# State-layer keys rotated by a permutation product, with new planner settings, in a three-layer decoder kernel

## The chip, the cores and the metric

The kernel runs on one NeuronCore of a Trainium2 chip. The metric is the device time of one execution in microseconds (us). The core has four compute engines that run their own instruction streams in order and wait for each other through semaphores: PE (TensorE, matrix products into PSUM), DVE (VectorE), ACT (ScalarE) and POOL (GpSimd). SP issues the transfers. PEld is the loading of PE's stationary operand.

## What is computed

Two batches of 512 tokens with 1024 features go through three layers, each added to its input after a layer norm:

```python
x = x + _L0_attn_ref(_layernorm(x), ...)               # 32 heads, binarised weights
x = x + _L0_xattn_ref(_layernorm(x), pos, ..., ctx)    # the state layer
x = x + _L0_ffn_ref(_layernorm(x), ...)                # dense with low-rank terms
```

The change lies in the state layer's attention. It reads three vectors of 256 features per token, projects them to queries, keys and values of 16 heads by 16 features, and rotates queries and keys by the token's position:

```python
def rope(x, pos):
    half = HD // 2
    ...
    x1, x2 = (x[..., :half], x[..., half:])
    return concatenate([x1 * cos - x2 * sin, x2 * cos + x1 * sin], axis=-1)
q, k = rope(q, pos), rope(k, pos)
scores = where(causal, einsum(q, k) / 4, -1e30); o = softmax(scores) @ v
```

After it, `rat_write` mixes the result into the token's 1024 features by a recurrence of exponentials and softplus, a second read feeds a gated product with `ctx`, and a second `rat_write` follows. The numbers are float32.

## The kernel before

**The planner.** The kernel is written as jobs (Python generators). A job yields an engine, an estimated duration and a ready time before it emits the instructions of a step. `run` (L453) picks, over and over, the job whose step could start first, where a job's lag (us) is added to that start: a low lag lets a job go first. The order in which steps are picked is the program order on every engine, which the hardware then keeps. The estimated durations and lags are no waits: they only set the order. The list in `build` (L1688) gives each job its lag and its needs, the marks in `self.when` that must have been planned before it may begin. `spawn` (L508) starts a sub-job with the parent's lag plus an entry of `LAGS` (L432), looked up as job.function, then function, then -0.3. `take` and `give` (L524) hand out rooms of buffers that all jobs share: 2 PSUM banks ("bank"), 3 PSUM pairs of banks ("pair"), 12 slabs, 4 probs, 8 pages, 11 rows.

**The stages.** In the order of the profile: the first layer's weights and projections; for batch A (0) and B (1) the score maxima (maxA, maxB) and the attention (attA, attB); the output product (outA, outB), which stores the residual in DRAM (`kept`). Then the state layer: state_inputs (stateA, stateB), the maxima of its causal scores (maxC, maxD), attention (attC, attD), and tails (tailA, tailB: both `rat_write`s and what is between them). Last, denseA and denseB. Jobs of both batches overlap.

**state_inputs** (L1109). For each of four tiles of 128 tokens it loads `kept`, measures mean and variance (`measured`, L982), normalises on DVE, keeps the mean and factor in `norm` for the tails (two more DVE instructions of 128x1), and calls `read` (L999), which transposes, multiplies by the read weights, normalises the three outputs of 256 (one DVE instruction each), transposes back and applies gain and bias (`gained`, L1078). Batch A reads "wide" through pairs and probs, batch B through banks. When all four tiles are read, twelve products follow, each into a bank: four groups of 128 slots for queries (kind 0), keys (kind 1) and keys of a third, slot-permuted weight (kind 2). A group has four heads of 32 slots; each head stands in four runs of 8. `rotated` (L1147) multiplies a bank by one of three tables (`rotation_table`, L954) on DVE; for kind 2 it then adds the result to the keys of kind 1. So a rotated key is (weight 1 product) x cos + (weight 2 product) x signed sin. Four value products end the stage.

**Maxima and attention.** `peaks` (L554) multiplies queries by keys and reduces maxima on DVE. `turned` (L592) splits each negative maximum into three bf16 parts by four small DVE instructions, transposes them on PE and copies them to a `shift` row on ACT. `attend` (L618) multiplies again, adds the shift by a product with `ones16`, and takes exponentials on ACT. In the first layer the probabilities are added up on DVE, except in a group's last step when `direct` (L734) is true, which `SPARE` governs.

**The end.** tail_weights (L1355) loads the tails' weights and `ctx`, tail (L1376) handles 128 tokens (at most three at once, the "lanes"), dense_weights (L1536) adds a low-rank product to the dense weights on PE and DVE, dense (L1583) handles 128 tokens of the last layer.

Of the kernel before, what the change touches and what calls it, by code (L numbers as in the profile page):

```python
# [18 lines left out]
P = 128  # L19
# [50 lines left out]
class Kernel:  # L70
# [79 lines left out]
    def constants(self):  # L150
        nc = self.nc
        self.ident = self.const([P, P], "ident")
        make_identity(nc, self.ident)
        self.ident16 = self.const([P, P], "ident16", BF16)
        nc.vector.tensor_copy(self.ident16, self.ident)
        self.ones = self.const([P, P], "ones")
        nc.gpsimd.memset(self.ones, 1.0)
        self.ones16 = self.const([P, P], "ones16", BF16)
        nc.gpsimd.memset(self.ones16, 1.0)

        self.late = []
# [12 lines left out]

        self.spread = self.const([P, P], "spread")
        nc.vector.tensor_copy(
            self.spread.rearrange("p (j i) -> p j i", j=4),
            self.ident.rearrange("p (j i) -> p j i", j=4)[:, :, 16:17].to_broadcast([P, 4, 32]),
        )
        self.eps = self.const([P, 1], "eps")  # L180
        nc.gpsimd.memset(self.eps, EPS)

        self.eye = self.const([P, 32], "eye")
        nc.vector.tensor_reduce(
            self.eye, self.ident.rearrange("p (j r) -> p r j", j=4), AX.X, ALU.add
        )
# [238 lines left out]
    def output_weights(self):  # L425
# [8 lines left out]
        "attB.added": 0.0, "attB.ahead": -0.3, "co.emptied": -0.1, "cv.emptied": -0.1, "denseA.emptied": -1.0,  # L434
        "denseA.stored": 1.0, "denseA.summed": -0.6, "denseB.emptied": 0.3, "denseB.stored": -2.0,
        "denseB.summed": -0.1, "emptied": -0.6, "exponentials": 0.3, "factor.put": -1.0, "finished": 0.0,
        "gained": -1.0, "gated": -1.0, "joined": -0.6, "k.scale_of": 0.0, "maxA.reduced": 0.0,
        "maxA.turned": -0.1, "maxB.reduced": 0.3, "maxB.turned": -0.3, "maxD.turned": -0.3, "outA.clean": 1.0,
        "outA.stored": 2.0, "outB.stored": -1.0, "proj0.featured": -1.0, "proj0.valued": -0.6,
        "proj1.featured": -1.0, "proj1.valued": -0.6, "q.scale_of": 0.0, "residual": 1.0, "rotated": 0.0,  # L440
        "stateA.emptied": -0.3, "stateA.rotated": -0.1, "stateB.gained": 0.0, "stateB.rotated": 0.0,
        "stored": 0.6, "summed": -0.6, "tableB.emptied": -2.0, "tailA.gained": -1.0, "tailA.residual": -2.0,
        "tailB.emptied": -0.6, "tailB.gained": -2.0, "tailB.gated": 0.0, "tailB.residual": 0.3,
        "v.scale_of": 0.0, "weights.joined": -0.1, "wo.scale_of": 0.0,
    }
    SPARE = 1
# [145 lines left out]
    def turned(self, name, b, g, mx, reduced, earlier):  # L592
        nc = self.io
        yield from self.join(*earlier)
        t = yield from self.join(*reduced)
        t = yield "DVE", 1.2, t
        parts = self.parts[self.flip]
# [4 lines left out]
        nc.vector.tensor_copy(parts[:, :, :, 1], rest)  # L602
        nc.vector.tensor_tensor(parts[:, :, :, 2], rest, parts[:, :, :, 1], ALU.subtract)
# [14 lines left out]
    def attend(self, groups, operands, scale, causal):  # L618
# [24 lines left out]
        def probabilities(g, kt):  # L643
# [10 lines left out]
            for j in range(4):  # L654
                r = slice(32 * j, 32 * j + 3)
                self.mm(
                    s[j // 2][:, j % 2, q0:], lhsT=self.ones16[r, :], rhs=shift[r, q0:], start=False, stop=True
# [340 lines left out]

    def read(self, x, t, w, gb, nout, dst, wide):  # L999
# [59 lines left out]
        t = yield "DVE", 0.42 * nout, t  # L1059
        for o in range(nout):  # L1060
            nc.vector.tensor_scalar(
                rows[o], rows[o], mv[:, o, 0:1], rstd[:, o : o + 1], ALU.subtract, ALU.mult
            )
# [30 lines left out]
    def state_weights(self):  # L1094
# [7 lines left out]
        self.proj = [w[0][:, 0], w[0][:, 1], w[1][:, 0]]  # L1102
# [6 lines left out]
    def state_inputs(self, b, wide):  # L1109
# [10 lines left out]
        def tile_of(q):  # L1120
# [24 lines left out]
        firsts = {}  # L1145

        def rotated(bank, kind, g, dst, t):  # L1147
            if dst is None:
                yield from self.join(firsts[g])
                t = max(t, (yield from self.take("row")))  # L1150
            t = yield "DVE", 0.69, t
            to = self.row([P, S]) if dst is None else dst[:, g, :]
            nc.vector.tensor_tensor(to, bank, table[:, kind, :], ALU.mult)
            self.give("bank", t)
            if dst is None:
                t = yield "DVE", 0.69, t
                nc.vector.tensor_tensor(kk[:, g, :], kk[:, g, :], to, ALU.add)
                self.give("row", t)
# [3 lines left out]
        for kind, (y, dst) in enumerate(((ys[0], qq), (ys[1], kk), (ys[1], None))):  # L1162
            w = self.proj[kind]
            for g in range(4):
                room = yield from self.take("bank")
                done = yield "PE", 1.9, max(t, room)
                bank = self.bank([P, S])
                self.accumulate(bank, [(w[:, i, g * P : (g + 1) * P], y[:, i, :]) for i in range(2)])
                job = self.spawn(rotated(bank, kind, g, dst, done))
                ends.append(job)  # L1170
                if kind == 1:
                    firsts[g] = job
# [515 lines left out]
    def build(self):  # L1688
# [39 lines left out]
                ("stateA", self.state_inputs(0, True), 0.2, "attB.scores"),  # L1728
# [62 lines left out]
def _layout(inputs):  # L1791
# [16 lines left out]
                _slots(qkv[1], (1, 0, 1, 0)),  # L1808
# [39 lines left out]
```

## Time and profile before

| | |
|---|---|
| median of 3 runs | 1129.61 us (1126.38 to 1132.65) |
| profiled execution | 1127.92 us |
| its span, first to last instruction | 1126.2 us |
| mean granted PE clock | 0.96 |

Times in the profile count from the first instruction. Where the stages lie (first to last instruction on PE, us):

| stage | PE | stage | PE |
|---|---|---|---|
| attB | 431 to 533 | maxD | 721 to 776 |
| outB | 533 to 592 | attD | 769 to 841 |
| stateA | 541 to 622 | tailA | 722 to 981 |
| stateB | 611 to 721 | weights | 842 to 859 |
| maxC | 622 to 668 | tailB | 877 to 1081 |
| attC | 661 to 709 | denseA, denseB | 868 to 1103, 982 to 1122 |

How to read the rows: a group row has the line of the code, engine, operation, what it writes and reads with shapes, the count, the busy time and the mean of one in ns, then the idle time of the engine before it with what ended it. A row of a timeline or of the chain begins with start and duration in us. A float32 product appears as two MATMUL records. Almost every instruction carries the line of a helper (L51, L130, L133, L142), so rows are told apart by tile names: `stateA_bank` is a PSUM bank of job stateA. A PE that is called busy is not at its peak, since the ends of products are modelled; the granted clock (1.00 is full) stands beside it.

### The profile page before, as it was taken

The page shows a single profiled execution, that of the slowest core. Times are in us where ns is not written, and L with a number is a line of the kernel's source. Part 1 is how long each engine was busy: PE and PEld are TensorE (multiplying, and loading weights), DVE is VectorE, ACT ScalarE, POOL GpSimd, SP SyncE. Part 2 cuts the span into 40 slices and gives each one's busy share as a digit, 9 for nine tenths or more (in the row PEclk, how much of TensorE's full clock was granted, in tenths as well). Part 3 has the DMA queues.
Part 4 walks back from the last instruction along what each step waited for, and adds up shares of the span by engine and source line. Part 5 has one row for each costly group of instructions (what it writes and reads, how often), then busy time and mean ns, then how long its engine had stood idle before and what let it go on. Part 6 is the DMA issues. An engine that isn't in the chain of part 4 may idle for free.

```text
span 1126.2 us, 16121 instructions
## 1 busy us (share of the span) xinstructions
PE 1056.2 (94%) x6364; PEld 520.5 (46%) x6364; DVE 840.2 (75%) x1391; ACT 443.9 (39%) x714; POOL 238.2 (21%) x249
## 2 busy tenths in 40 slices
PE   4889999999999998999999899989988999998998
PEld 3554353333233632332554553546455466664643
DVE  8978888578888856787877972499758778687751
ACT  6762101388600214787121256225753233432210
POOL 3542333411321403364452012001210000000000
PEclk8999999999998998999999899969999999987999
DMA  6621000100214221150012200510131101111100
GB/s 255 211 78 29 20 10 20 29 20 23 63 38 145 118 75 38 31 199 1 28 68 74 94 1 1 228 38 1 51 144 50 50 7 57 38 38 38 38 19 38
DMA packets 25520, 70.51 MB, mean 63 GB/s; under 512 B 5330, under 2 KB 5348, under 8 KB 24548
## 3 DMA queue, kind: packets, MB, share of 16 engines
q1 hardware_dynamic: 25444, 69.48, 18.0%
q8 instruction: 50, 0.82, 0.3%
q14 instruction: 26, 0.21, 0.1%
HBM read 50.59 MB, written 10.49 MB: 54 GB/s over the span
## 4 chain that ended last, share of the span: by engine, by line
PE 78%; DVE 13%; ACT 5%; issue 2%; DMA 1%; POOL 1%; SPq 0%; DVEq 0%; ACTq 0%; POOLq 0%
PE proj_bank L130 8%; PE denseA_pair L130 6%; PE denseB_pair L130 5%; PE outA_bank L130 4%; PE attA_pair L130 4%; PE attB_pair L130 4%; PE tailA_bank L130 4%; PE attA_bank L130 3%; PE attB_bank L130 3%; PE maxB_pair L130 3%; PE maxA_pair L130 3%; PE outB_bank L130 3%; PE stateB_bank L130 3%; PE tailB_bank L130 3%; PE factor_bank L130 3%; PE tailA_pair L130 2%
## 5 line engine op out<-in xcount | busy, mean ns | idle before, releaser
L51 DVE TENSOR_REDUCE maxB_mx<-maxB_pair 128x2 f32<-128x1024 f32 x64 | 75.4, 1219 | 21.2 <-PE maxB_pair L130 21.0
L51 DVE TENSOR_REDUCE maxA_mx<-maxA_pair 128x2 f32<-128x1024 f32 x64 | 75.6, 1216 | 14.1 <-PE maxA_pair L130 14.1
L130 PEld LDWEIGHTS <-start_slab 128*128 128x128 bf16 x480 | 45.0, 99 | 69.8 <-issue 22.9
L51 DVE TENSOR_TENSOR attB_probs<-attB_probs,attB_probs 128x1024 f32<-128x1024 f32 x46 | 62.7, 1401 | 12.8 <-PE attB_bank L130 7.1
L51 ACT ACTIVATE attB_probs<-attB_pair 128x1024 f32<-128x1024 f32 x64 | 62.6, 1023 | 20.2 <-PE attB_pair L130 10.1
L51 DVE TENSOR_TENSOR attA_probs<-attA_probs,attA_probs 128x1024 f32<-128x1024 f32 x46 | 56.8, 1283 | 16.8 <-ACT attA_probs L51 9.8
L51 ACT ACTIVATE attA_probs<-attA_pair 128x1024 f32<-128x1024 f32 x64 | 62.0, 1021 | 9.8 <-PE attA_pair L130 9.4
L130 PE MATMUL proj_bank<-in_slab,start_slab 128*128 128x512 bf16 x240 | 57.0, 388 | 1.6 <-ACT in_slab L51 1.6
L130 PE MATMUL proj_bank<-in_probs,start_slab 128*128 128x512 bf16 x240 | 54.7, 380 | 0.0
L130 PE MATMUL maxB_pair<-maxB_row,proj_slab 32*128 32x512 f32 x256 | 47.9, 691 | 3.1 <-DVE maxB_mx L51 3.1
L51 POOL TENSOR_SCALAR proj_row<-proj_row 128x512 f32<-128x512 f32 x24 | 48.1, 2006 | 1.9
L130 PE MATMUL outA_bank<-wo_slab,attA_slab 128*128 128x512 bf16 x192 | 47.6, 398 | 0.7 <-ACT maxB_shift L51 0.7
L130 PE MATMUL attB_pair<-proj_slab,attB_row 32*128 32x512 f32 x256 | 46.9, 686 | 0.0
L51 ACT ACTIVATE proj_row<-proj_bank,cs 128x512 f32<-128x512 f32 x20 | 13.7, 686 | 81.8 <-PE proj_bank L130 61.2
L130 PE MATMUL outB_bank<-wo_slab,attB_slab 128*128 128x512 bf16 x192 | 43.3, 380 | 0.3 <-POOL attB_slab L51 0.3
L130 PE MATMUL attA_pair<-proj_slab,attA_row 32*128 32x512 f32 x256 | 41.6, 639 | 0.3 <-ACT attA_probs L51 0.3
L130 PE MATMUL attB_bank<-attB_probs,proj_slab 128*32 128x512 f32 x256 | 37.6, 619 | 1.1 <-DVE tableA_slab L51 0.7
L51 ACT COPY maxB_shift<-maxB_bank 128x512 bf16<-128x512 bf16 x8 | 4.7, 585 | 85.9 <-PE maxB_bank L133 85.9
L51 POOL TENSOR_SCALAR proj_slab<-proj_row 128x512 f32<-128x512 f32 x24 | 14.8, 616 | 107.7 <-ACT proj_row L51 89.1
L130 PE MATMUL maxA_pair<-maxA_row,proj_slab 32*128 32x512 f32 x256 | 36.8, 640 | 0.0
L51 POOL TENSOR_SCALAR_AFFINE_SELECT attD_probs<-attD_probs 128x512 f32<-128x512 f32 x16 | 12.0, 750 | 114.7 <-ACT attD_probs L51 105.2
L51 POOL TENSOR_SCALAR outA_row<-outA_row 128x512 f32<-128x512 f32 x16 | 21.4, 1340 | 65.0 <-DVE outA_row L51 60.8
(411 smaller groups left out, 2297.3 us busy)
## 6 DMA issues: line engine op xcount, KB each, us to landing
in_page<-in_x_dram SPq DMA_DIRECT2D x8, 512.0 KB, 3.9
q_page<-in_q_weight_dram SPq DMA_DIRECT2D x8, 512.0 KB, 5.4
wo_page<-in_o_weight_dram SPq DMA_DIRECT2D x8, 512.0 KB, 3.6
tailW_slab<-in_write_dram SPq DMA_DIRECT2D x3, 752.0 KB, 10.9
maxA_row<-proj_slab SPq DMA_DIRECT2D x32, 64.0 KB, 2.0
attA_row<-proj_slab SPq DMA_DIRECT2D x32, 64.0 KB, 2.0
maxB_row<-proj_slab SPq DMA_DIRECT2D x32, 64.0 KB, 2.0
outA_page<-in_x_dram SPq DMA_DIRECT2D x4, 512.0 KB, 3.8
```

The source lines that it names most:

```text
L51: return self.kernel.pin(getattr(self.engine, name)(*args, **kw))
L130: self.pin(self.nc.tensor.matmul(*args, **kw))
```

## The change

- The third key weight, its load and its four products per batch go. `keyed` takes its place: ACT copies the raw keys from the bank to a row, DVE multiplies the same bank by the cos table, PE multiplies the row by a 128x128 permutation `swap` (halves of each 16 slots exchanged) into another bank, DVE multiplies this by the sin table and adds it. Keys are computed first, queries after.
- `keep` (the `norm` pair) moves from DVE, after the normalisation, to POOL, before it. The normalisations go through `standard` with other estimated durations.
- `turned` splits the positive maximum; the sign moves to the constant: `minus16` for `ones16`.
- `LAGS`, `SPARE`, and lags and needs of jobs change.

```diff
@@ constants
-        self.ones16 = self.const([P, P], "ones16", BF16)
-        nc.gpsimd.memset(self.ones16, 1.0)
+        self.minus16 = self.const([P, P], "minus16", BF16)
+        nc.gpsimd.memset(self.minus16, -1.0)
...
+        self.swap = self.const([P, P], "swap")
+        halves = [t.rearrange("p (e h i) -> p e h i", h=2, i=8) for t in (self.swap, self.ident)]
+        for h in range(2):
+            nc.vector.tensor_copy(halves[0][:, :, h, :], halves[1][:, :, 1 - h, :])
@@ LAGS, only entries that differ
-        "denseA.emptied": -1.0, "denseA.stored": 1.0, "denseB.stored": -2.0, "denseB.summed": -0.1,
-        "rotated": 0.0, "stateA.rotated": -0.1, "stateB.rotated": 0.0,
-        "tailA.residual": -2.0, "tailB.gained": -2.0, "tailB.gated": 0.0,
+        "denseA.emptied": -2.0, "denseA.stored": -2.0, "denseB.stored": -0.1, "denseB.summed": -2.0,
+        "maxD.reduced": -0.3, "stateA.gained": -0.3,
+        "tailA.residual": 0.6, "tailB.gained": -0.1, "tailB.gated": -0.3,
-    SPARE = 1
+    SPARE = 100
@@ turned
-        nc.vector.tensor_scalar(parts[:, :, :, 0], mx, -1.0, None, ALU.mult)
-        nc.vector.scalar_tensor_tensor(rest, mx, -1.0, parts[:, :, :, 0], ALU.mult, ALU.subtract)
+        e.tensor_copy(parts[:, :, :, 0], mx)
+        e.tensor_tensor(rest, mx, parts[:, :, :, 0], ALU.subtract)
...
@@ new
+    def standard(self, parts, n, t):
+        t = yield "DVE", (0.15 + n / 1500) * len(parts), t
+        for x, mean, r in parts:
+            self.io.vector.tensor_scalar(x, x, mean, r, ALU.subtract, ALU.mult)
+        return t
@@ state_weights
-        for kind in range(3):
+        for kind in range(2):
             t = yield from self.fetch(self.proj[kind], a["proj"][:, kind], 512)
@@ state_inputs, tile_of
-            t = yield "DVE", 1.3, t
-            nc.vector.tensor_scalar(x, x, mv[:, 0, 0:1], r, ALU.subtract, ALU.mult)
             keep = self.small([P, 2], "norm", bufs=8)
-            nc.vector.tensor_copy(keep[:, 1:2], r)
-            nc.vector.tensor_scalar(keep[:, 0:1], mv[:, 0, 0:1], r, -1.0, ALU.mult, ALU.mult)
+            yield "POOL", 0.4, t
+            nc.gpsimd.tensor_copy(keep[:, 1:2], r)
+            nc.gpsimd.tensor_scalar(keep[:, 0:1], mv[:, 0, 0:1], r, -1.0, ALU.mult, ALU.mult)
+            t = yield from self.standard([(x, mv[:, 0, 0:1], r)], D, t)
@@ state_inputs, rotation
+        def keyed(bank, g, t):
+            tr = max(t, (yield from self.take("row")))
+            tr = yield "ACT", 0.59, tr
+            raw = self.row([P, S])
+            nc.scalar.copy(raw, bank)
+            t = yield "DVE", 0.69, t
+            nc.vector.tensor_tensor(kk[:, g, :], bank, table[:, 1, :], ALU.mult)
+            self.give("bank", max(t, tr))
+            room = yield from self.take("bank")
+            tr = yield "PE", 0.97, max(tr, room)
+            other = self.bank([P, S])
+            self.mm(other, lhsT=self.swap, rhs=raw, start=True, stop=True)
+            t = yield "DVE", 1.38, max(t, tr)
+            nc.vector.tensor_tensor(raw, other, table[:, 2, :], ALU.mult)
+            self.give("bank", t)
+            nc.vector.tensor_tensor(kk[:, g, :], kk[:, g, :], raw, ALU.add)
+            self.give("row", t)
+            return t
...
-        for kind, (y, dst) in enumerate(((ys[0], qq), (ys[1], kk), (ys[1], None))):
+        for kind, y in ((1, ys[1]), (0, ys[0])):
@@ build, lags and needs
-                ("stateA", self.state_inputs(0, True), 0.2, "attB.scores"),
+                ("stateA", self.state_inputs(0, True), 0.2, "attB.7"),
...
-                ("maxD", self.peaks_2(1, "stateB"), 0.5, "stateB", "attC.scores"),
-                ("tailW", self.tail_weights(), -0.5, "attC", "stateB"),
+                ("maxD", self.peaks_2(1, "stateB"), 0.5, "stateB"),
+                ("tailW", self.tail_weights(), -1.0, "attC"),
                 ("tailA", self.tails(0), 0.5, "attC", "tailW"),
-                ("attD", self.attend_2(1, "maxD"), 0.2, "maxD.1"),
-                ("weights", self.dense_weights(), -1.0, "attD"),
-                ("tailB", self.tails(1), 0.2, "attD", "tailW", "tailA.1"),
-                ("denseA", self.dense_all(0, "tailA"), 0.5, "tailA.0"),
-                ("denseB", self.dense_all(1, "tailB"), 0.5, "tailB.0"),
+                ("attD", self.attend_2(1, "maxD"), 0.2, "maxD", "attC"),
+                ("weights", self.dense_weights(), 0.5, "attD"),
+                ("tailB", self.tails(1), 0.0, "attD", "tailW", "tailA.1"),
+                ("denseA", self.dense_all(0, "tailA"), 0.2, "tailA.0"),
+                ("denseB", self.dense_all(1, "tailB"), 0.2, "tailB.0"),
```

More of the change, by code (lines that the diff above doesn't have):

```diff
@@ L433 @@
         "added": 0.0, "ahead": 0.0, "attA.ahead": -0.1, "attA.exponentials": -0.1, "attA.finished": 0.3,
-        "attB.added": 0.0, "attB.ahead": -0.3, "co.emptied": -0.1, "cv.emptied": -0.1, "denseA.emptied": -1.0,
-        "denseA.stored": 1.0, "denseA.summed": -0.6, "denseB.emptied": 0.3, "denseB.stored": -2.0,
-        "denseB.summed": -0.1, "emptied": -0.6, "exponentials": 0.3, "factor.put": -1.0, "finished": 0.0,
+        "attB.added": 0.0, "attB.ahead": -0.3, "co.emptied": -0.1, "cv.emptied": -0.1, "denseA.emptied": -2.0,
+        "denseA.stored": -2.0, "denseA.summed": -0.6, "denseB.emptied": 0.3, "denseB.stored": -0.1,
+        "denseB.summed": -2.0, "emptied": -0.6, "exponentials": 0.3, "factor.put": -1.0, "finished": 0.0,
         "gained": -1.0, "gated": -1.0, "joined": -0.6, "k.scale_of": 0.0, "maxA.reduced": 0.0,
[L438 to L444, printed above, removed]
+        "maxA.turned": -0.1, "maxB.reduced": 0.3, "maxB.turned": -0.3, "maxD.reduced": -0.3,
+        "maxD.turned": -0.3, "outA.clean": 1.0, "outA.stored": 2.0, "outB.stored": -1.0,
+        "proj0.featured": -1.0, "proj0.valued": -0.6, "proj1.featured": -1.0, "proj1.valued": -0.6,
+        "q.scale_of": 0.0, "residual": 1.0, "stateA.emptied": -0.3, "stateA.gained": -0.3,
+        "stateB.gained": 0.0, "stored": 0.6, "summed": -0.6, "tableB.emptied": -2.0, "tailA.gained": -1.0,
+        "tailA.residual": 0.6, "tailB.emptied": -0.6, "tailB.gained": -0.1, "tailB.gated": -0.3,
+        "tailB.residual": 0.3, "v.scale_of": 0.0, "weights.joined": -0.1, "wo.scale_of": 0.0,
     }
-    SPARE = 1
+    SPARE = 100
     def run(self, jobs):
@@ L596, in turned @@
         t = yield "DVE", 1.2, t
+        e = nc.vector
         parts = self.parts[self.flip]
@@ L599, in turned @@
         rest = self.small([P, NT, 4], "rest")
-        nc.vector.tensor_scalar(parts[:, :, :, 0], mx, -1.0, None, ALU.mult)
-        nc.vector.scalar_tensor_tensor(rest, mx, -1.0, parts[:, :, :, 0], ALU.mult, ALU.subtract)
-        nc.vector.tensor_copy(parts[:, :, :, 1], rest)
-        nc.vector.tensor_tensor(parts[:, :, :, 2], rest, parts[:, :, :, 1], ALU.subtract)
+        e.tensor_copy(parts[:, :, :, 0], mx)
+        e.tensor_tensor(rest, mx, parts[:, :, :, 0], ALU.subtract)
+        e.tensor_copy(parts[:, :, :, 1], rest)
+        e.tensor_tensor(parts[:, :, :, 2], rest, parts[:, :, :, 1], ALU.subtract)
         room = yield from self.take("bank")
@@ L656, in probabilities @@
                 self.mm(
-                    s[j // 2][:, j % 2, q0:], lhsT=self.ones16[r, :], rhs=shift[r, q0:], start=False, stop=True
+                    s[j // 2][:, j % 2, q0:], lhsT=self.minus16[r, :], rhs=shift[r, q0:], start=False, stop=True
                 )
@@ L1058, in read @@
         mv, rstd, t = yield from self.measured([[r] for r in rows], t)
[L1059 to L1063, printed above, removed]
+        t = yield from self.standard([(rows[o], mv[:, o, 0:1], rstd[:, o : o + 1]) for o in range(nout)], 256, t)
         yn = yn.rearrange("p o a c h -> p (o a c h)")
@@ L1101, in state_weights @@
         w = [self.slab([P, 2, 2, 512]) for _ in range(2)]
-        self.proj = [w[0][:, 0], w[0][:, 1], w[1][:, 0]]
+        self.proj = [w[0][:, 0], w[0][:, 1]]
         self.values = w[1][:, 1].rearrange("p a b -> p (a b)")[:, :512].rearrange("p (a b) -> p a b", a=2)
-        for kind in range(3):
+        for kind in range(2):
             t = yield from self.fetch(self.proj[kind], a["proj"][:, kind], 512)
@@ L1144, in state_inputs, with queried @@
         table = self.table[b]
[L1145 to L1150, printed above, removed]
+        def queried(bank, g, t):
             t = yield "DVE", 0.69, t
-            to = self.row([P, S]) if dst is None else dst[:, g, :]
-            nc.vector.tensor_tensor(to, bank, table[:, kind, :], ALU.mult)
+            nc.vector.tensor_tensor(qq[:, g, :], bank, table[:, 0, :], ALU.mult)
             self.give("bank", t)
[L1155 to L1158, printed above, removed]
+            return t
[16 more added lines that the diff above has]
+            self.give("row", t)
             return t
         ends = []
-        for kind, (y, dst) in enumerate(((ys[0], qq), (ys[1], kk), (ys[1], None))):
-            w = self.proj[kind]
+        for kind, y in ((1, ys[1]), (0, ys[0])):
             for g in range(4):
@@ L1167, in state_inputs @@
                 bank = self.bank([P, S])
+                w = self.proj[kind]
                 self.accumulate(bank, [(w[:, i, g * P : (g + 1) * P], y[:, i, :]) for i in range(2)])
[L1169 to L1172, printed above, removed]
+                ends.append(self.spawn((keyed if kind else queried)(bank, g, done)))
         self.give("probs", done)
@@ L1807, in _layout @@
                 _slots(qkv[1], (0, 1, 0, 1)),
-                _slots(qkv[1], (1, 0, 1, 0)),
             ],
```

## The prediction

> **What bounds the kernel now.** I read the totals first, then the chain of waits, then a table of busy time by stage with the granted TensorE clock, and only then single rows.
>
> ```profile
> PE 1056.2 (94%) x6364; PEld 520.5 (46%) x6364; DVE 840.2 (75%) x1391; ACT 443.9 (39%) x714; POOL 238.2 (21%) x249
> ...
> PE 78%; DVE 13%; ACT 5%; issue 2%; DMA 1%; POOL 1%; SPq 0%; DVEq 0%; ACTq 0%; POOLq 0%
> ```
>
> TensorE (PE) is busy 94% of the span and holds 78% of the chain. The table by stage (start:end, length, busy time of PE, PEld, DVE, ACT, POOL, granted clock, DMA share, GB/s) shows where that fails:
>
> ```profile
> 592.00:622.00 30.00, 28.17 (x95) 15.05 (x94) 21.67 (x41) 4.79 (x14) 6.25 (x5) 1.00 0.26 87
> 622.00:661.00 39.00, 35.23 (x290) 22.78 (x288) 37.30 (x83) 11.71 (x30) 0.00 (x0) 0.91 0.17 56
> 661.00:709.00 48.00, 45.19 (x366) 16.96 (x366) 14.41 (x31) 29.25 (x51) 11.63 (x20) 1.00 0.07 21
> 709.00:722.00 13.00, 13.00 (x45) 7.00 (x44) 7.36 (x12) 2.29 (x6) 0.00 (x0) 1.00 0.99 403
> 722.00:776.00 54.00, 49.87 (x310) 27.89 (x307) 45.67 (x96) 16.08 (x31) 1.57 (x2) 0.81 0.06 24
> ...
> 842.00:877.00 35.00, 29.53 (x178) 18.79 (x177) 30.29 (x54) 12.05 (x24) 0.39 (x2) 0.95 0.22 75
> ```
>
> 592 to 622 is stateA's projections, 661 to 722 stateB's (first beside attC, then alone): there PE is full at full clock and DVE has room (14.41 of 48). 622 to 661 (maxC) and 722 to 776 (maxD) are the reverse: DVE is full, PE starves, and the clock falls to 0.91 and 0.81. So work taken from PE counts in the first kind of stage, an earlier or later start in the second.
>
> **The third weight.** Each batch loses four bank products (kind 2) and gains four `swap` products.
>
> ```profile
> 599.11 12.28 PE stateA_bank L130 x28
> ```
>
> 28 records in 12.28 us are 0.439 us each, back to back. The 48 records of stateA's 12 banks are four to a bank, so a bank costs 1.75 us; a swap is one product, two records, 0.88 us. Eight times (1.75 - 0.88) is **-7.0 us**. The Trainium skill, "TensorE: Matmul & The Clock Gate", section "Back-to-back issue gap", gives about 131 ns as the sustained spacing of 512-column matmuls and 216 ns for an isolated one. Two passes to a record would make 0.26 and 0.43: by the sustained figure the saving is an estimated 4.2 us, by the row 7.0. The row is this very product, so I take 7.0.
>
> **Its price: banks.** There are two PSUM banks. Before, a product held one for 1.75 plus one DVE multiply (0.69 in the rows of `stateB_slab`). Now ACT copies the raw keys (the 128x512 PSUM copies of attB took 0.58) and DVE multiplies the same bank. Do these two run together? The nearest place is the tails' `bank`, where DVE reads 8 columns and ACT 256 others:
>
> ```profile
> 728.63 0.17 DVE L51 COPY tailA_few<-tailA_bank 128x8 f32<-128x8 f32 x1 [1.03 <-PE tailA_bank L130]
> 728.83 0.37 ACT L51 COPY tailA_row<-tailA_bank 128x256 f32<-128x256 f32 x1 [3.13 <-DVE tailA_few L51]
> ```
>
> ACT starts when DVE ends, and its wait is put down to DVE though it needs none of DVE's data. The Trainium skill ("PSUM — Partial Sum Buffer", section "PSUM bank collisions raise a hardware error") speaks against the change here: two engines may not touch one bank and quadrant at once, two readers included. So a raw bank is held 1.75 + 0.58 + 0.69 = 3.0 us and its swap's bank 0.88 + 0.69 = 1.6: 4.6 us of bank time per group. (Side by side, as separate banks would allow, it would be 4.0.) Over two free banks that is 2.3 us against 2.63 of PE, so PE stays the bound and the cost is 0. With one bank held, by attC's accumulation or stateB's transposes, 4.6 against 2.63 loses 2.0 per group, 8 groups 16 us. Ends 0 and +16; I take **+2**, one group in eight, because the old products also had to share banks and PE showed only 2.81 us idle from 661 to 709. ACT's eight copies (4.7 us) lie beside PE; ACT is busy 29.25 of 48 there. DVE keeps its count: twelve multiplies and four adds a batch. Keys now come first and queries last, so the longer key chain drains behind four query products (7.0 us) and the values.
>
> **Small edits, together.** The load of the third weight goes (512 KB, one SP issue; landing took 6.4 us, beside attB): 0. `keep` moves two DVE instructions of 0.15 and 0.20 us, eight times, to POOL: 2.8 us less DVE, which counts only in DVE-full stages. Nobody but the tails' ACT rescale reads them, 100 us later; behind them in POOL's queue stand outB's cleaning and attC's masks. No row shows a 128x1 POOL operation; nearest are the 0.1 us memsets below and the 0.8 us copies of the tables above: 0. `turned` keeps four DVE instructions (0.20, 0.18, 0.20, 0.23), and minus16 costs what ones16 cost: 0. `SPARE` does nothing: seven groups with six adds and a last one with four are the 46 in the rows, so no group but the last was ever direct. `maxD.reduced` at -0.3 is the default. The planner's new durations for `standard` change no instruction. Two copies for `swap` come early on DVE: the eyes copies (1.0 us each, half as wide) end at 3.1 and DVE's first input work is at 4.7; 0 to +1, I take **+0.3**.
>
> **stateA from attB.7.** Group 7's first step is planned some two steps of about 3.2 us before the last scores. The first page load was issued at 492.5, so data is there; what is late is DVE's first statistics at 536.84. From 525 to 540 PE's busy time is 13.77 of 15 with DVE 9.25, and maxC's DVE work, now from 622, could begin while outB still has PE work to hide it. The gain is at most the seven microseconds of the shift, at worst zero plus what attB's tail loses when DVE (21.5 of 25 busy from 500 to 525) serves stateA first; its lag of 0.2 against -1.0 keeps attB ahead. -7 to +4, I take **-3**. Next late then is DVE in maxC.
>
> **maxD, tailW, attD.** maxD loses its need for attC.scores. The last scores of attC ran at 703.4 and stateB ended at 722.1: this wait did not end last, 0. tailW is freed of stateB, but its loads already landed under stateB (DMA share 0.99 from 709 to 722): 0. Its SP waits stand ahead of the tails' page loads only, as before. attD now waits for all of maxD and not maxD.1:
>
> ```profile
> 769.46 1.50 PE L130 MATMUL attD_pair<-stateB_slab,stateB_slab 32*128 32x512 f32 x5
> ...
> 777.84 0.57 ACT L51 COPY maxD_shift<-maxD_bank 128x512 bf16<-128x512 bf16 x1
> ```
>
> maxD.1's shift was ready at 752.1, 17 us before attD began, so the old need was slack. The new one is ready at 778.4, 9.0 us after the old start. Queued behind attD are its ACT exponentials, then the dense weights, then dense. PE has two 3.8 us blocks of tailA to run meanwhile, and 842 to 877 has 5.5 us idle to take what moves: 0 to +9, I take **+2**.
>
> **Lags of tails and dense.** Dense goes from level with tailA (0.5) to ahead (0.2), the weights from -1.0 to 0.5, tailB to 0.0. Idle PE plus lost clock from 842 to 877 is 5.5 + 1.8, from 982 to the end 9.9 + 11.5 by the same table (134.09 busy of 144, clock 0.92): 29 us in all. Long dense runs (1.72 us per four records, little DVE) offered earlier fill such holes; a later tailA.3 and later weights open others. -12 to +14, I take a tenth of the hole, **-3**.
>
> **Sum.** The profiled execution took 1127.92 (span 1126.2 and 1.7 around it; the median shown is 1129.61, 1.7 above). -7.0 + 2 + 0.3 - 3 + 2 - 3 = -8.7, hence 1119.2: **1119 us**.
>
> **Rivals.** (a) *Banks eat the saving.* Half of the 16 us comes true, +8 for +2, and the shift of stateA brings nothing: 1128. For: two banks, serial readers. Against: PE full in every stage with products. (b) *The starved stages close too.* The shift brings 5 for 3 and the holes give 9 for 3: 1119 - 2 - 6 = 1111. For: 29 us of hole. Against: DVE's sum hardly falls. (c) *Slower: dense comes late.* Place: 842 to 877. The weights, formerly straight behind attD (842.0 to 859.4 on PE), wait behind attD's 9.0 us and then, at lag 0.5, behind tail blocks of some 10 us. PE then has 19 us with tails alone, as from 722 to 776, where busy share times clock was 0.92 x 0.81 = 0.75: a quarter, 4.8, is lost, and the 9.0 of attD go unfilled. The late tailA.3 leaves its dense (16 products of 0.86, 13.8 us) with little beside it, of which I count a third, 4.6. 1127.9 - 7.0 + 2 + 0.3 + 18.4 = 1142. It decides if the first dense product, now at 872.5, comes 10 us or more later.
>
> The clock speaks for (c): [...]740 to 755 ran at 0.50 with PE called busy 12.7 of 15. [...]by the row it loses half: 7.5 us in those 15. I price by the row.
>
> **How the numbers follow.** This measurement can tell about 0.5% from no change, so the bounds are 1124 and 1135. Forecast 0.48, (b) 0.19, (a) 0.13, (c) 0.20. The forecast's own range is 1113 to 1126, mostly below 1124: faster 0.67, same 0.13, slower 0.20. The range over all, 1105 to 1139, leaves out half of (c) and a quarter of (b).
>
> **What would show it.** Right: per batch 32 projection records and 8 of the swap where 48 stood; each state's projections 3 us shorter or more; ACT copies directly ahead of DVE multiplies; DVE's first stateA statistics before 533; attD's first product after maxD's last shift. Wrong: PE gaps over 0.5 us between swap and raw products, a clock below 0.8 after 780, or a first dense product after 882.

## The result and the profile after

| | before | after |
|---|---|---|
| median (20 runs each, one chip) | 1129.8 us (1125.7 to 1133.6) | 1135.05 us (1129.5 to 1138.9) |
| profiled execution | 1127.92 | 1136.26 |
| its span | 1126.2 | 1134.5 |

The ratio is 1.0040, interval 1.0024 to 1.0056: slightly slower, where 1119 us was forecast. The two profiled executions lie 8.3 us apart and the medians 5.3, so some 3 us of what the profiles show below belong to these two executions. The first row of the page, then the table by stage of the profile after (start:end, length, busy PE, PEld, DVE, ACT, POOL, granted clock, DMA share, GB/s):

```profile
PE 1059.1 (93%) x6315; PEld 524.4 (46%) x6348; DVE 844.6 (74%) x1385; ACT 444.6 (39%) x714; POOL 242.5 (21%) x265
```

```profile
592.00:618.00 26.00, 24.80 (x82) 11.62 (x81) 16.46 (x28) 2.91 (x7) 8.92 (x9) 1.00 0.20 70
618.00:658.00 40.00, 35.35 (x267) 20.62 (x260) 35.31 (x74) 10.22 (x25) 1.08 (x4) 0.83 0.15 48
658.00:701.00 43.00, 40.05 (x395) 18.54 (x393) 18.17 (x43) 31.84 (x58) 11.96 (x22) 1.00 0.11 36
701.00:722.00 21.00, 19.91 (x53) 9.40 (x52) 11.91 (x18) 3.89 (x9) 0.20 (x1) 1.00 0.72 261
722.00:776.00 54.00, 49.05 (x304) 27.95 (x304) 43.61 (x93) 13.65 (x27) 0.00 (x0) 0.81 0.09 34
776.00:849.00 73.00, 66.22 (x523) 37.68 (x522) 48.98 (x95) 45.05 (x81) 12.08 (x19) 0.98 0.10 33
849.00:884.00 35.00, 29.63 (x159) 19.68 (x158) 29.71 (x52) 12.20 (x24) 0.39 (x2) 0.84 0.34 129
```

Against the same table before: stateA's stage is 4 us shorter. The two starved stages (maxC, maxD) have stayed, with a clock of 0.83 where it was 0.91, and 0.81 as before. Where the time went is seen best between the last PE instructions of the stages (us; every kernel of this study is set into this table by its own profiled execution):

| | attB to stateA | stateA to stateB | stateB to attD | attD to the end |
|---|---|---|---|---|
| before | 88.4 | 99.7 | 119.5 | 285.4 |
| after | 82.9 | 104.4 | 127.0 | 285.7 |
| difference | -5.5 | +4.7 | +7.5 | +0.3 |

With attB ending 1.3 later, that is the +8.3 of the span. The first column looks like the saving, but some 4 us of PE's work in it are stateB's first reading products, which ran between stateA's (611 to 622) before and now come behind its end. By stateB's end 0.8 us of gain is left, and attD costs far more than that.

The swap itself runs as forecast. A piece of the timeline of the profile after (start, duration, engine, line, what; in brackets the idle time before it and its releaser):

```profile
700.42 0.59 ACT L51 COPY stateB_row<-stateB_bank 128x512 f32<-128x512 f32 x1 [1.30 <-PE stateB_bank L130]
701.04 0.69 DVE L51 TENSOR_TENSOR stateB_slab<-stateB_bank,tableB_slab 128x512 f32<-128x512 f32 x1 [3.75 <-ACT stateB_row L51]
...
701.79 1.13 PE L130 MATMUL stateB_bank<-stateB_row,swap 128*128 128x512 f32 x2 [0.54 <-DVE stateB_slab L51]
...
702.95 0.69 DVE L51 TENSOR_TENSOR stateB_row<-stateB_bank,tableB_slab 128x512 f32<-128x512 f32 x1 [1.22 <-PE stateB_bank L130]
```

DVE begins on the raw keys 0.03 us after ACT ends on the same bank and is released by ACT, as `tailA_few` and `tailA_row` were before. PE waits 0.54 us for a bank here (more than 0.5 was a sign of being wrong in the prediction). In all PE is idle 0.6 us more in stateA's stretch than before, and 1.1 us from attC's end to stateB's, where it was not idle at all.

The rows that answer to attD's wait and to stateA's start, also from the timeline after:

```profile
538.14 1.28 DVE L51 BATCH_NORM_STATS2 stateA_st<-stateA_page 128x6 f32<-128x512 f32 x2
...
775.81 3.79 PE L130 MATMUL tailA_pair<-tailA_row,tailW_probs 128*128 128x128 f32 x32
...
778.78 0.57 ACT L51 COPY maxD_shift<-maxD_bank 128x512 bf16<-128x512 bf16 x1
...
779.53 1.12 PE L130 MATMUL attD_pair<-stateB_slab,stateB_slab 32*128 32x512 f32 x2
...
782.54 0.71 PE L130 MATMUL attD_pair<-stateB_slab,stateB_slab 32*128 32x512 f32 x3 [1.89 <-DVE tailA_page L51]
```

stateA's first statistics are no earlier (536.84 before), and attD begins 10 us later than its 769.46 of before, 0.2 us behind the end of maxD's last shift. It does not wait for that shift alone: on PE a block of 32 of tailA's products stands just ahead of it. Its next scores then wait 1.89 us for DVE, which is still reading tailA's products.

### The profile page after: what moved, and what is told of

It is laid out like the page before. It is cut to its first block, busy times and chain, and to the rows that moved or that the text cites. A ratio compares the mean times of both kernels' runs of the same rounds, so it can differ in the third digit from the quotient of the medians.

```text
span 1134.5 us, 16081 instructions
## 1 busy us (share of the span) xinstructions
PE 1059.1 (93%) x6315; PEld 524.4 (46%) x6348; DVE 844.6 (74%) x1385; ACT 444.6 (39%) x714; POOL 242.5 (21%) x265
## 5 line engine op out<-in xcount | busy, mean ns | idle before, releaser
L51 ACT ACTIVATE attB_probs<-attB_pair 128x1024 f32<-128x1024 f32 x64 | 62.6, 1023 | 20.2 <-PE attB_pair L130 10.1
```

Of the source, the lines that this page charges most:

```text
L51: return self.kernel.pin(getattr(self.engine, name)(*args, **kw))
```

## The experiments

Eighteen kernels were run, each beside the kernel before on the same chip (1127 to 1130 us there). Letters of theories are those of the expectations. Below, "work" is the time that PE is busy less half of what it is busy at half clock, "lost clock" that half, "idle" the rest; all three are added up from the records and the granted clock of a profile. A single profile is uncertain by some 2 us in a stretch: e1, e3 and e4 have one and the same order on PE up to stateB's end, and took 110.8, 112.4 and 108.2 us from stateA's end to stateB's.

### Which part costs: e1 to e4, e8, e12

e1 is the kernel before with the rotation alone (two weights, `keyed` and `queried`, the swap constant).

> The kernel before with the permutation of raw keys alone, all settings and the reading of the inputs as before. Theory R (the reading order is the loss: in the changed kernel stateB's reading is pushed behind maxC and attC runs without stateB's products beside it): here stateB reads as before, so about two thirds of the 7 us of PE work come through, 1125 us. Theory K (the key chain with its two bank visits is itself the loss): 1130 us or more. Theory D (attD's new wait is the loss): the full saving, 1123 us.

Measured: 1136.22 us, ratio 1.0079 (1.0052 to 1.0105). The rotation alone makes the kernel slower. stateA is done 5.4 us sooner (83.0), but stateA to stateB takes 110.8 instead of 99.7. By its number this is theory K, but not by its cause: from attC's end to stateB's, where most of B's keys are made, PE is idle only 0.5 of 19.2 us.

e2 is the changed kernel with attD's need put back:

```
-  ("attD", self.attend_2(1, "maxD"), 0.2, "maxD", "attC"),
+  ("attD", self.attend_2(1, "maxD"), 0.2, "maxD.1"),
```

> The changed kernel with attD needing maxD.1 again, nothing else. Theory D: attD starts near 770 again, the dense weights and denseA come 8 to 15 us earlier, and the time falls by 8 us to 1127. Theories R and K: holes in PE elsewhere take it up, 1133 to 1136.

Measured: 1164.05, ratio 1.0320 (1.0297 to 1.0343). Up to attD's end 6.7 us are won, but the planner then puts the whole tail in another order, and attD to the end takes 321.7 instead of 285.7.

e3 is the changed kernel with state_inputs' reading as before: the normalisation's planned durations, `keep` on DVE, no `stateA.gained` lag.

```
-            yield "POOL", 0.4, t
-            nc.gpsimd.tensor_copy(keep[:, 1:2], r)
...
+            nc.vector.tensor_copy(keep[:, 1:2], r)
...
-  ... "stateA.gained": -0.3,
```

> The changed kernel with the reading of the state inputs as before (norm pair on DVE, its planned durations, no lag entry for stateA's gain), so that 82 of stateB's products again stand before maxC's last and outB before stateA's projections; all else changed. Theory R: attC has stateB's work beside it again, time falls by 5 us or more to 1129. Theories K and D: within 2 us of the changed kernel, 1134 to 1136.

Measured: 1164.67, ratio 1.0321 (1.0296 to 1.0346). Worse in every stretch but the first: 112.4, 137.9 and 299.8. Theory R had forecast the opposite for the second stretch, and falls.

e4 is e3 with attD's need and the weights' lag (-1.0) of before as well.

> e3 with attD needing maxD.1 and the dense weights at lag -1.0 as before; the other lags and needs as changed. Theories R and D together: both losses gone, the 7 us come through, 1121 us. Theory K: the banks still cost, 1130 us.

Measured: 1163.52, ratio 1.0304 (1.0271 to 1.0337). These undoings cost 28 us and more against the changed kernel, much of it behind attD: e2 +36.0, e3 +14.1, e4 +23.9 in the last column. The lags of tails and dense seem to fit one arrival of attD and no other, so later runs are compared up to attD's end.

e8 is the kernel before with attD's wait alone (`"maxD.1"` becomes `"maxD"`).

> The kernel before with attD needing all of maxD instead of its second group, nothing else. Theory W (the wait itself costs): stateB's end to attD's end grows from 119.5 to 125-128 us. Rival: the wait is hidden by tailA's products, which are put there in its place, the stretch stays within 2 us of 119.5 and the changed kernel's 127.0 comes of its clock or of stateB's late keys. The tail keeps its order of ends (tailA, tailB, denseA, denseB), so the run should be 1127 plus the wait less what tailA's earlier products give back: 1126-1134.

Measured: 1148.01, ratio 1.0162 (1.0126 to 1.0197). stateB to attD takes 130.7 for 119.5, more than theory W had, and the run lies above its 1126 to 1134. From the timeline of e8:

```profile
779.13 3.79 PE L130 MATMUL tailA_pair<-tailA_row,tailW_probs 128*128 128x128 f32 x32
...
781.03 0.57 ACT L51 COPY maxD_shift<-maxD_bank 128x512 bf16<-128x512 bf16 x1
...
782.86 1.72 PE L130 MATMUL attD_pair<-stateB_slab,stateB_slab 32*128 32x512 f32 x5
```

attD comes behind the last shift and behind a block of tailA's products, as in the changed kernel. Of the +11.3, 4.5 are idle, 4.8 lost clock and 1.9 work: tailA's products, put into the gap, do not fill it.

e12 is the changed kernel with the third weight in place of the swap product.

> The changed kernel with the third projection weight back in place of the swap product, all else as changed (settings, norms, waits). If the rotation saves its 5-7 us of TensorE work in the end as well, under these settings: 1140-1143. If it is neutral or costs, as with the rotation alone: 1127-1136. In either case attB's end to stateA's end goes back from 83 to 88 us, and stateB's end to attD's end stays near 127, since attD's wait stays; the tail is ordered anew by the planner (tailA, tailB, denseA, denseB as before), which alone was worth 14 to 36 us in earlier runs, so the three stretches up to attD's end are to be compared rather than the span.

Measured: 1159.19, ratio 1.0259 (1.0224 to 1.0294). attB to stateA took 83.8, not the 88 expected, since stateB's reading stays behind stateA's end in these settings; stateA to stateB took 106.4 and stateB to attD 131.4. The run is above both forecasts; behind attD's end it took some 13 us more than the changed kernel.

Together these give the time from attB's end to attD's end by three parts of the change (us). before, e8 and e1 have the other lags and needs of before, the rest those of the changed kernel (e4 has the weights' lag of before too), so only steps within one of these groups are clean:

| rotation | reading | attD waits for all of maxD | |
|---|---|---|---|
| third weight | before | no | 307.6 (before) |
| third weight | before | yes | 320.6 (e8) |
| swap | before | no | 313.6 (e1), 311.0 (e4) |
| swap | before | yes | 333.2 (e3) |
| swap | changed | no | 307.6 (e2) |
| third weight | changed | yes | 321.5 (e12) |
| swap | changed | yes | 314.3 (after) |

With the changed reading and the wait the rotation is worth -7.2 us (321.5 to 314.3), the size of the forecast. That is luck for the most part: 2.9 us of it are there at stateB's end, and the other 4.4 come between stateB's end and attD's, where the rotation takes no product away but the planner has put PE's work in another order. With the reading of before it costs 6.0 (before to e1); across the groups, 3.4 (e4), or 12.6 with the wait. The wait costs 6.7 at its cheapest (307.6 to 314.3), 13.0 in the kernel before, about 20 with the swap and the old reading (e3 against e1 or e4). So the parts can't be added up; the wait is dear in every row.

### What takes the saving back between stateA and stateB: e5 to e7, e9 to e11, e13 to e18

In PE's account from attB's end to stateB's end the saving is there throughout, and something else fills it (runs with one order on PE up to stateB's end stand together):

| | length | work | idle | lost clock |
|---|---|---|---|---|
| before | 188.1 | 174.0 | 10.8 | 3.4 |
| e8 (order of before) | 189.8 | 174.0 | 9.1 | 6.8 |
| e12 (third weight, changed settings) | 190.2 | 173.3 | 11.9 | 5.1 |
| e1 (swap alone) | 193.8 | 166.2 | 12.3 | 15.2 |
| e3 (order of e1) | 195.2 | 166.0 | 12.3 | 16.9 |
| e4 (order of e1) | 191.2 | 168.8 | 14.1 | 8.3 |
| after | 187.3 | 167.8 | 13.5 | 6.1 |
| e2 (order of after) | 186.1 | 168.4 | 13.2 | 4.5 |

So one order gives the work to within 3 us, and its lost clock differs by up to 8.6 from one execution to the next.

**The order of stateB's products.** In e1 and after, stateB's products run alone behind attC (19.2 and 20.9 us from attC's end to stateB's, 12.4 before). e5 is the changed kernel with maxC's lag 0.5 -> 0.7, e6 is e1 with the same, e18 the changed kernel with 0.8, which leaves PE's order behind attD exactly as it is.

> The changed kernel with one number altered: the lag of maxC 0.5 -> 0.7, so that stateB's last reading is put ahead of maxC's last reductions; by the program order 11 of stateB's 20 projection and swap products then stand before attC's last scores (0 in the changed kernel, 10 of 24 before). Theory O (the saving of the rotation is given back because stateB's reading slides behind maxC and its products run alone after attC): stateA's end to stateB's end falls from 104.4 to 99 us or less, the run to 1128-1131. Theory G (the halved clock in maxC, whatever the order, costs it): the stretch stays at 103-106 and the run at 1133-1137. Theory K (the chain copy, swap, multiply, add of a key is what stateB waits for): the same as G, with the 20 products taking as long per key wherever they stand.

> The kernel before with the rotation alone, and maxC's lag 0.5 -> 0.7: 16 of stateB's 20 products before attC's last scores (2 of 20 with the rotation alone). Theory O: stateA's end to stateB's end falls from 110.8 to 102 us or less, the run from 1136 to 1126-1129 against 1127 before. Theory G or K: the stretch stays above 107 and the run at 1132-1137.

> The changed kernel with maxC's lag 0.5 -> 0.8: 16 of stateB's 20 products before attC's last scores, and from attD's last product on the same order as the changed kernel has (at 0.7 it had another). Theory L (TensorE is busy without a gap from attC's start to stateB's end, so products put beside attC only make attC end later; the tail's weights and kept rows are loaded into what attC frees, and TensorE, in its order, waits for them with maxD's products behind): attC ends at 714-720 instead of 700.9, stateB within 5 us of 721.8, TensorE idle for 6-10 us between 720 and 745 for tailA's rows, stateB's end to attD's end 135-143 instead of 127.0, the run 1143-1152. Theory O (products beside attC are a gain): stateB ends at 712-717 and the run is 1127-1131.

Measured: e5 1164.52, ratio 1.0305 (1.0270 to 1.0340); e6 1144.93, 1.0131 (1.0100 to 1.0162); e18 1161.04, 1.0288 (1.0236 to 1.0339). stateA to stateB took 111.1, 102.4 and 107.4; only e6's stretch did what theory O said, and its run did not. The next stage shows why: stateB to attD took 142.0, 133.1 and 144.4. The busy table of e18, then its waits, of PE and of ACT (engine, what waited, for what: us in total, times, longest):

```profile
720.00:745.00 25.00, 12.19 (x57) 7.81 (x57) 4.18 (x11) 5.95 (x8) 0.19 (x1) 0.73 0.69 233
```

```profile
PE tailA_bank L133 <- ACT tailA_row L51: 12.8, 1, 12.8
...
ACT tailA_slab L51 <- DMA tailA_slab<-kept: 12.6, 1, 12.6
```

PE is busy half of these 25 us (23.64 in the changed kernel). It stands at tailA's first tile, which waits for ACT, which waits for the load of `kept`; this load is issued behind those of the tails' weights, for which attC's end frees the room. maxD's products, ready, are queued behind tailA's on PE. attC ended at 720.0 instead of 701.2, since in the changed kernel PE has next to no gap from 658 to 722 (clock 1.00, 60 of 64 us busy): a product put beside attC only moves attC's end. Theory L is borne out, with a larger stall than it expected, and O falls.

**The halved clock.** In e7 every mask product of maxC and maxD in e1 is done three times; in e9 and e11 only those of some groups; e10 is the kernel before with those of maxD's first two groups done twice.

```
                         for jj in range(2):
-                            self.mm(s[pr][:, jj, qt * P : nk], lhsT=self.ident16, rhs=self.late[0], start=False, stop=True)
+                            for last in [False] * 2 + [True]:
+                                self.mm(s[pr][:, jj, qt * P : nk], lhsT=self.ident16, rhs=self.late[0], start=False, stop=last)
```

> The kernel before with the rotation alone, and each causal mask product of maxC and maxD done three times (the added -1e30 leaves the maxima as they are): 8 more 128-column products for each tile of queries in stages where VectorE is the bound, some 6-13 us of more TensorE work in each of the two stages, the order of everything else the same. Theory G: the clock stays whole from 627 to 668 us, stateA's end to stateB's end falls from 110.8 to 104 or less and the run by 5 us or more, to 1131 or less. Theory O: the stretch stays at 109-114, since stateB's products come after attC as before, and the run at 1134-1142.

> The kernel before with the rotation alone, and the mask products of maxC's first group of heads (of four) done three times: 32 more products of 128 columns, at the 0.09 us each that the run with all of them tripled added (11.6 us for 128), 2.9 us of TensorE work between 615 and 630 us; order as with the rotation alone. Theory G (a light stretch of TensorE at 624 us lets the clock fall for 20 us, and that takes back what the rotation saves): the clock stays whole from 627 to 647, stateA's end to stateB's end falls from 110.8 to 102-105, the run from 1136 to 1127-1131. Theory O (the order of stateB's reading, not the clock): the stretch stays at 108 or more.

> The kernel before, and the mask products of maxD's first two groups done twice: 32 more products, some 2.9 us, where its clock is at half from 738 to 759 us (9.1 us lost in stateB's end to attD's end, by the busy time of TensorE at half clock). Theory G: the half clock is shortened by 10 us or more, that stretch falls from 119.5 to 115-118 and the run by 2-5 us, below both kernels: 1122-1126. If the clock falls all the same, the products cost their own time and the run is 1128-1131.

> The rotation alone, with the mask products thrice in maxC's first group and in maxD's first two: 96 more products, 8.6 us of work. Theory G: both stretches keep the clock, stateA's end to stateB's end 102-105, stateB's end to attD's end 115-119 (119.8 with the rotation alone), the run 1123-1129. Otherwise the added work is paid: 1136-1142.

Measured: e7 1138.26, ratio 1.0086 (1.0063 to 1.0110); e9 1139.67, 1.0091 (1.0061 to 1.0122); e10 1129.86, 1.0005 (0.9985 to 1.0025); e11 1138.87, 1.0079 (1.0057 to 1.0102). The busy tables of e1 and then e7, from stateA's end to attC's start:

```profile
615.00:660.00 45.00, 41.89 (x288) 25.23 (x287) 38.82 (x89) 11.60 (x29) 0.00 (x0) 0.75 0.23 71
```

```profile
617.00:661.00 44.00, 40.80 (x414) 27.61 (x413) 38.50 (x89) 11.58 (x29) 0.00 (x0) 1.00 0.20 70
```

The clock went from 0.75 to 1.00 and the stretch did not move: 45.4 us in e1, 44.3 in e7, 46.5 in e9. The added products take the place of the lost clock (in e7 11.6 us more work from stateA to stateB, 15.2 less lost). So these runs do not say what a whole clock without them would give, nor whether PE's rate is what this stretch waits for. In e9 and e11 the clock fell in this stretch in spite of the added products, and in e10 the half clock came as before, for 20.5 us from 741, so these three do not test theory G. It stays without support: no run got below the kernel before by way of the clock. A weak sign against it is e4, which has e1's order and lost 6.9 us less of the clock up to stateB's end, but came only 2.6 us sooner.

**VectorE.** It was idle only 1.8 of the 39.1 us of this stretch before (5.9 of 45.4 in e1). In e13 (e1), e14 (before) and e15 (after) the normalisations of stateB go to ACT, every other instruction keeping its place; e16 takes maxC's full-width maxima in e1 twice; e17 is e13 with e9's masks.

```
+            if b:
+                nc.scalar.activation(x, x, AF.Identity, scale=keep[:, 1:2], bias=keep[:, 0:1])
```

> The kernel before with the rotation alone, and the normalisation of stateB's four tiles (1.0 us each on VectorE) done by ScalarE with the kept scale and bias; every other instruction in its place. Theory V (from stateA's end to attC's start VectorE is the bound, so that the earlier end of stateA is lost there, whatever TensorE and its clock do): VectorE is relieved of 3 tiles' worth in that stretch, attC's first product comes 2-4 us sooner than 660.3 and the run falls by 2-4 us, to 1132-1134. Theory P (TensorE is the bound there, by its halved clock or by its order): attC's first product stays within 1 us and the run at 1135-1138.

> The kernel before with the same four normalisations on ScalarE, all else in its place. Theory V: VectorE is idle for 1.8 of the 39.1 us there, so attC's first product comes 2-4 us before 660.6 and the run falls by 2-4 us against 1127-1130: this version would beat both kernels. Theory P: no change (within 1.5 us).

> The changed kernel with the same four normalisations on ScalarE, all else in its place. VectorE does less of stateB's reading in that stretch here (15.5 us against 24.1 before), one or two tiles: attC's first product 1-2 us before 658.3, and stateB's last reading, which ends 18 us before stateB does, sooner by as much: the run 1131-1134 by theory V, 1134-1137 by P.

> The rotation alone, with the full-width row maxima of maxC (8 of its 32 reductions, 1.17 us each) taken twice: 9.4 us more of VectorE's work in maxC, all else in its place. Theory V: attC's first product comes 6-9 us later than 660.3, and the run is 6-9 us longer, 1142-1145. Theory P: VectorE's idle 5.9 us in that stretch take most of it, attC's first product is at most 4 us later and the run 1136-1140.

> The rotation alone, with both reliefs at once: the normalisations of stateB on ScalarE (as in the run with these alone) and the mask products of maxC's first group done three times (2.9 us of TensorE work). Theory V+G (VectorE and the halved clock each take over when the other is relieved, so that only both together shorten the stretch): from stateA's end to attC's start 40-42.5 us instead of 45.4, the run at 1129-1132. Otherwise (the chain from scores to maxima to the next scores through the pair banks sets it, and neither engine's rate): 44-47 us, and the run at 1134-1140.

Measured: e13 1134.99, ratio 1.0057 (1.0037 to 1.0077); e14 1131.09, 1.0011 (0.9995 to 1.0027); e15 1133.49, 1.0050 (1.0032 to 1.0067); e16 1146.13, 1.0186 (1.0149 to 1.0223); e17 1136.32, 1.0071 (1.0053 to 1.0089). The same stretch in the busy tables of e13, e14, e16 and e17:

```profile
615.00:660.00 45.00, 40.79 (x287) 24.36 (x285) 38.68 (x88) 14.45 (x32) 0.00 (x0) 0.77 0.21 69
```

```profile
621.00:662.00 41.00, 37.50 (x290) 23.73 (x289) 35.88 (x83) 14.05 (x32) 0.00 (x0) 0.83 0.17 59
```

```profile
616.00:672.00 56.00, 45.73 (x288) 27.53 (x287) 47.60 (x96) 11.68 (x30) 0.00 (x0) 0.72 0.18 55
```

```profile
615.00:662.00 47.00, 42.96 (x321) 26.91 (x320) 38.97 (x88) 15.07 (x32) 0.00 (x0) 0.79 0.22 68
```

More of VectorE's work lengthens the stretch by as much (e16: 9 us more, attC's first product 11 us later). Less of it shortens nothing (attC's first product: e13 0.5 us sooner than e1, e14 1.5 later than before, e15 0.4 later than after), not even with more masks beside it (e17). In e14 the clock fell instead, from 0.91 to 0.83. So V fits e16 and P fits e13 to e15, and neither fits all of them; V in its plain form falls. Whether PE would shorten the stretch at a whole clock without added work stays open. No version beat both kernels; e10 and e14 are level with the one before.

**What the traces leave.** DVE and PE hand pieces to each other there: scores to maxima, pages to turns, turns to copies. What the traces do show is that attC starts no sooner for the rotation: its first product comes 127.4 us after attB's last one before and 128.4 in e1, and with the changed settings 124.3 in e12 and 123.9 in the changed kernel. All of the 5.4 us by which e1's stateA ends sooner are gone by then. One thing that could hold it is when stateB's reading can begin. SyncE's queue and the first statistics, from the timelines of before, e1 and after:

```profile
587.36 12.82 SPq L142 DMA_DIRECT2D kept<-outB_page  x2
600.35 19.42 SPq L142 DMA_DIRECT2D stateB_page<-kept  x4
605.17 1.27 DVE L51 BATCH_NORM_STATS2 stateB_st<-stateB_page 128x6 f32<-128x512 f32 x2
```

```profile
585.98 16.03 SPq L142 DMA_DIRECT2D kept<-outB_page  x2
602.18 13.46 SPq L142 DMA_DIRECT2D stateB_page<-kept  x4
606.96 1.28 DVE L51 BATCH_NORM_STATS2 stateB_st<-stateB_page 128x6 f32<-128x512 f32 x2 [0.27 <-DMA stateB_page<-kept]
```

```profile
590.53 19.23 SPq L142 DMA_DIRECT2D kept<-outB_page  x2
609.92 11.55 SPq L142 DMA_DIRECT2D stateB_page<-kept  x4
614.74 1.28 DVE L51 BATCH_NORM_STATS2 stateB_st<-stateB_page 128x6 f32<-128x512 f32 x2
```

The load of B's rows is issued behind outB's last store, and outB has nothing to do with the keys. With the rotation stateA ends 5 us sooner and stateB's reading starts no sooner, or 9.6 us later in the changed kernel, where outB's last product ends at 602.3 instead of 591.8, with 8 of stateA's 20 projection and swap products put ahead of it. That would make the freed time empty, with maxC alone unable to fill PE. But no run moved that load, so it is not shown. Nor can it be the whole of it: in the changed kernel the load comes 9.6 us later and attC still starts 2.2 us sooner than before (658.7 for 660.9), with less of stateB ahead of it (68 of its 176 records on PE, 114 of 184 before).

## Why the prediction was wrong, point by point

- **The third weight, -7.0.** As PE's work this is near: -6.2 after, -5.2 to -8.0 in the three profiles of e1's order, by the account above, at 0.44 us per record as the row had it. What failed is the step to the path: "work taken from PE counts in the first kind of stage". Between stateA's products and stateB's lies a stage of the second kind. From attB's end to stateB's, idle time and lost clock together grew by 5.4 (after) or 13.3 (e1; 8.2 in e4), so that 0.8 us came of the 6.2, and less than nothing in e1. In e1 10.1 of the 13.3 lie between stateA's end and maxC's last product; in the changed kernel only 2.6 of the 5.4, and the rest is spread in pieces of the size of the noise. The table in the prediction said that this stage starves; what an earlier stateA would find to do there was not asked. The runs show that the work was saved and that attC started no sooner for it; what holds that start stays open. With the changed settings on both sides (e12 to after) 7.2 us are there at attD's end, but 4.4 of them not by the saved products.
- **Banks, +2.** Near. The serial readers are there; PE's idle time in stateA's stretch rose by 0.6 us (4.2 to 4.8), and 1.1 us were idle from attC's end to stateB's. Rival (a), which had the banks eat the saving, is wrong in its cause.
- **The small edits, 0.** The failed reading was "The planner's new durations for `standard` change no instruction". They change none, but, with the move to POOL and the lag of stateA's gain, they change the order: undoing them (e3) brings stateA to stateB from 104.4 back to 112.4. With the swap they helped, so at 0 they were mis-sized the other way; which of the three did it was not tried.
- **stateA from attB.7, -3.** Wrong. With or without this edit every engine gets the same instructions in the same order, so it is worth exactly 0; the sign asked for (first statistics before 533) did not come (538.14).
- **maxD, tailW.** 0 was kept for both, and no run undid either edit. For tailW it can hold only as attC ends early; e18 shows what its loads cost when attC ends late.
- **attD's wait, +2.** The term next to the third weight in the size of its miss. It is +7.5 in its stage, +6.7 by e2, +13.0 in e8; only the end of 9 that the prediction kept for its range was of the right order, and e8 is past it. tailA's blocks were named as cover. In e8 idle and lost clock together rose by 9.3 in spite of them: DVE is busy 46.20 of the 55 us from 724 to 779, 24.9 of them with maxD's maxima, and tailA needs DVE too. That this is why the cover failed is argued, not tried.
- **Lags of tails and dense, -3.** The stretch behind attD came to +0.3. Rival (c)'s deciding event came (first dense product 889.0 for 872.4, 16.6 later), its price did not: 849 to 884 ran at a clock of 0.84 for 0.95, and from 982 to the end PE was busy 143.39 of 152.5 at 0.98 instead of 134.09 of 144.2 at 0.92. Late dense was paid at once and won back at the end. So the direction of (c) came true by the lost saving and by one part of its sum, "the 9.0 of attD go unfilled" (7.5 in its stage); the other part, 9.4 for late weights and dense, had come to nothing by the end. The starved stages of (b) did not close either: maxC's clock fell to 0.83.

With the stretches as measured: -5.5 + 4.7 + 7.5 + 0.3, and 1.3 by which attB ended later.

## What to carry to other kernels

Work that is taken from a full engine is worth its time only up to the next stage that is bound by something else; ask there what the earlier start will find ready, and which load or store that input stands behind. A wait that lets a whole stage pass first costs the overlap of both, and filler that needs the same second engine does not give it back. Order settings can be fitted to one arrival: undoing one or two here cost 28 us, so compare stretches of the trace and not the ends.

## What the runs showed of the hardware

- The halved clock is not bound to a PE that the records call idle. In e1 PE ran at 0.50 for 20.5 us from 627.6, and from 615 to 660 it is called busy for 41.89 of 45 us (2.63 of the 3.40 us just before the clock fell); in e7, with 128 more products of 0.09 us in this stage, the clock stayed at 1.00. In e10 32 more products in maxD changed nothing. Away from the ends of the traces the half clock came in multiples of 3.4 us, up to 20.5 in these stages and 23.9 in e4's tail (from 1015).
- Two readers of one bank, ACT and DVE, ran one behind the other in the new place too, 0.03 us apart (701.01 to 701.04 after), though neither needs the other's data.
